# The fc products of a cross-attention block, split twice into seven: quarters of quarters for three of four groups

## The chip, the cores and the metric

The kernel runs on one core of a Trainium2 chip. The metric is the time of one launch on the device in microseconds, as the median of several runs. A separate profiled execution gives the trace from which the lines below are taken; its span is the time from its first to its last instruction. TensorE is called PE in the profile, its weight loads PEld, VectorE DVE, ScalarE ACT and GpSimd POOL; SP is the engine that issues almost all transfers. All data are fp32.

## What is computed

There are B = 8 sequences of 256 tokens with D = 512 features, a context of the same shape, 16 heads of 32, and an inner width of 2048.

```
x   = layer_norm(hidden) ;  q = x @ q_w + q_b ;  k, v = enc @ k_w + k_b, enc @ v_w + v_b
att = softmax(q k^T / sqrt(32) + mask) v
hidden = att @ cproj_w + cproj_b + hidden
y   = layer_norm(hidden)
out = hidden + gelu(y @ fc_w + fc_b) @ proj_w + proj_b
```

The change concerns the last two lines only, and of those above all y @ fc_w, a product of a 512-token group [512 x 512] with fc_w [512 x 2048].

## The kernel before

The sequences are worked through in NG = 4 groups of two sequences, that is 512 tokens. The first half of the kernel does attention for all groups; it ends at about 356 us of the trace, and nothing in it is changed but the order in which three pieces of fc_w are asked for. The second half, the `with ExitStack() as mlp` block, runs group by group: fc with gelu, then proj, then the next group. The order of all instructions on each engine is the order in which the Python code issues them (`tc.manual_schedule`); each engine works through its own queue strictly in that order, and semaphores hold an instruction until what it reads is written and what it overwrites has been read.

Large matrix products are done in Winograd's form of Strassen's method. Both operands are cut into four quarters, four sums of quarters are formed for each (`A_SUMS` on weights: s1, which takes the place of "21", s2, s3, s4; `B_SUMS` on activations: t1, t2, t4 and one that takes the place of "12"), and the four quarters of the result come from seven products instead of eight. The seven products of an operand pair are, in the order in which they are issued: ("11","11") into bank 1, ("s2","t2") into bank 6, ("s3","12") into bank 7, ("21","t1") into bank 5, then ("12","21") added into bank 1, ("22","t4") added into bank 7 and ("s4","22") added into bank 5. u1 is a copy of bank 1 on ScalarE after the first product; u2 = bank 6 + u1, u3 = bank 7 + u2, and the quarters 22, 12 or 21 are bank + u, all on VectorE. Because banks 1, 7 and 5 are added into a second time, their first contents must have been read before the second product may start in them.

In the fc part (`for q in range(HF // 2)`), fc_w lies in four pieces `fcw[q]` (tag "w", four buffers), loaded once; each piece has its seven weight operands in SBUF. For each q there are seven products of four matmuls, each of a 128x128 weight tile and 256 moving columns, all recorded under line 922, the helper `mm`; every such fp32 matmul is two instructions in the trace, so 4 x 7 x 4 x 2 = 224 per group. The names in the profile are pf for these results and fcw and y for their operands. Gelu (line 985) goes from the bank or from h into h; h holds the quarters "11", "12", "21", "22" and "s3" as lists of four tiles.

The proj part is one more Strassen product per group, h times proj_w, with seven products of 16 matmuls (results py, weights pw and pw_t). Its sums over h are made on GpSimd (lines 1026, 1027, 1078 and 1087). Between the proj products the next group's normalised tokens are transposed (pyt, lines 216 and 244, `turn_next`), and its `B_SUMS` are made on VectorE (line 171). The output grows in `ht` (named resm), which starts as the residual, and is stored by `store`.

Of the kernel before, what the change touches and what calls it, by code (L numbers as in the profile page):

```python
# [16 lines left out]
P = 128  # L17
# [5 lines left out]
def tile_xattn_block(  # L23
# [225 lines left out]
    with ExitStack() as att:  # L249
# [549 lines left out]
        for q in range(3):  # L799
            begin(g, 0, 3, load_fc, q)  # L800
# [105 lines left out]
    with ExitStack() as mlp:  # L906
        wpool = mlp.enter_context(tc.tile_pool(name="mlpw", bufs=1, reuse_waits="tile"))
        work = mlp.enter_context(tc.tile_pool(name="mlpwork", bufs=2, reuse_waits="tile"))
# [5 lines left out]
        )  # L914

# [5 lines left out]
        def mm(ps, lhsT, rhs, first, last):  # L921
            nc.tensor.matmul(ps, lhsT, rhs, start=first, stop=last, skip_group_check=True)  # L922

# [5 lines left out]
        def sum_pw():  # L929

            for to, a, b, op in (
# [5 lines left out]
                for p in range(0, HF, 2):  # L937
                    c = slice(p, p + 2)
                    nc.vector.tensor_tensor(pw[to][:, c], pw[a][:, c], pw[b][:, c], op)
                    yield  # L940
# [3 lines left out]
        nc.gpsimd.tensor_tensor(pbd, projb[:, :HD2], projb[:, HD2:], ALU.subtract)  # L944

        for g in range(NG):
            y = ys[g]

            h = {
                n: [  # L950
                    work.tile([P, 2, S], F32, tag=f"h{n}", bufs=HF // 2, name=f"h{n}_{g}_{q}")
                    for q in range(HF // 2)
                ]
                for n in ("11", "12", "21", "22", "s3")
            }

            def fc(bank, w, b, q, first, last):
                for i in range(2):
                    for c in range(HC):
                        mm(  # L960
                            bank[:, i, :],
                            fcw[q][w][:, c, ts(i, P)],
                            y[b][:, c, :],
                            first and i == 0 and c == 0,
                            last and c == HC - 1,
                        )
# [5 lines left out]
            def by_tiles(row):  # L972
                return row[:, None, :].to_broadcast([P, 2, HD2])

            for q in range(HF // 2):
                bank = {
                    n: ps_f.tile([P, 2, S], F32, tag=f"f{n}", name=f"pf{n}_{g}_{q}") for n in (1, 6, 7, 5)
                }
                u1 = work.tile([P, 2, S], F32, tag="u1", bufs=1, name=f"u1_{g}_{q}")
                u2 = work.tile([P, 2, S], F32, tag="u2", bufs=2, name=f"u2_{g}_{q}")  # L980
                u3 = work.tile([P, 2, S], F32, tag="u3", bufs=1, name=f"u3_{g}_{q}")

                def gelu(n, half, src):
                    for i in range(2):
                        nc.scalar.activation(  # L985
                            h[n][q][:, i, :],
                            src[:, i, :],
                            AF.Gelu_apprx_tanh,
                            bias=col(c_fcb, half * HF + 2 * q + i),
                            scale=1.0,  # L990
                        )

                ahead = g == 0 and q + 1 < HF // 2

                def some_pw(n):
                    if g == 0 and q:
                        for _ in range(n):
                            next(pw_sums)

                fc(bank[1], "11", "11", q, True, False)  # L1000
                nc.scalar.copy(u1, bank[1])  # L1001
                fc(bank[6], "s2", "t2", q, True, True)
                nc.vector.tensor_tensor(u2, bank[6], u1, ALU.add)
                fc(bank[7], "s3", "12", q, True, False)
                nc.vector.tensor_tensor(u3, bank[7], u2, ALU.add)
                fc(bank[5], "21", "t1", q, True, False)
                nc.vector.tensor_tensor(h["22"][q], bank[5], u3, ALU.add)
                if ahead:
                    sum_up(nc.gpsimd, fcw[q + 1], A_SUMS, 0, 1)
                some_pw(1)  # L1010
                fc(bank[1], "12", "21", q, False, True)

                gelu("11", 0, bank[1])
                gelu("22", 1, h["22"][q])
                fc(bank[7], "22", "t4", q, False, True)
                nc.vector.tensor_tensor(h["12"][q], bank[7], u2, ALU.add)
                if ahead:
                    sum_up(nc.gpsimd, fcw[q + 1], A_SUMS, 2, 3)
                some_pw(2)
                gelu("12", 1, h["12"][q])  # L1020
                fc(bank[5], "s4", "22", q, False, True)
                nc.vector.tensor_tensor(h["21"][q], bank[5], u2, ALU.add)  # L1022
                some_pw(1)
                gelu("21", 0, h["21"][q])

                nc.gpsimd.tensor_tensor(h["s3"][q], h["11"][q], h["21"][q], ALU.subtract)  # L1026
                nc.gpsimd.tensor_tensor(h["21"][q], h["21"][q], h["22"][q], ALU.add)
                if q == 0:
                    ht = residual(work, hid_dram[g], "resm", f"resm_{g}")
                    if g + 1 < NG:  # L1030
                        load_hid(g + 1)
# [6 lines left out]
            if g + 1 < NG:  # L1038
                seen, roots, normalise = layer_norm(hids[g + 1], f"m{g + 1}")
                for f in (*seen, roots, *normalise):  # L1040
                    f()
# [108 lines left out]
```

## Time and profile before

| quantity | value |
| --- | --- |
| median of 3 runs | 754.42 us (753.89 to 755.68) |
| the profiled execution: time, span | 754.31 us, 752.5 us |
| fc of group 0, of group 1, of group 2 | 48.35, 48.34, 48.35 us |
| proj of group 0, of group 1 | 50.30, 50.21 us |
| bytes moved by DMA | 68.70 MB |

Busy time on PE counts overlapping matmuls once, so a PE that is always busy need not be at its best pace. In the rows of groups, the number after x counts instructions, then come the busy time in microseconds and the mean nanoseconds of one, then the idle time of the engine just before them with what ended it. The duration of a matmul runs from its issue to its last result; matmuls overlap, so the time between two starts is shorter.

### The profile page before, as it was taken

The page shows a single profiled execution, that of the slowest core. Times are in us where ns is not written, and L with a number is a line of the kernel's source. Part 1 is how long each engine was busy: PE and PEld are TensorE (multiplying, and loading weights), DVE is VectorE, ACT ScalarE, POOL GpSimd, SP SyncE. Part 2 cuts the span into 40 slices and gives each one's busy share as a digit, 9 for nine tenths or more (in the row PEclk, how much of TensorE's full clock was granted, in tenths as well). Part 3 has the DMA queues.
Part 4 walks back from the last instruction along what each step waited for, and adds up shares of the span by engine and source line. Part 5 has one row for each costly group of instructions (what it writes and reads, how often), then busy time and mean ns, then how long its engine had stood idle before and what let it go on. Part 6 is the DMA issues. An engine that isn't in the chain of part 4 may idle for free.

```text
span 752.5 us, 12116 instructions
## 1 busy us (share of the span) xinstructions
PE 744.8 (99%) x4437; PEld 626.2 (83%) x4437; DVE 360.5 (48%) x969; ACT 293.1 (39%) x852; POOL 380.0 (50%) x346
## 2 busy tenths in 40 slices
PE   9999999999999999999999999999999999999997
PEld 7888777888888877778888888888888888888886
DVE  3676755676466566765355542245422355122111
ACT  2276777766676777761341002330013300032100
POOL 3856779577564478996654421136202165012540
PEclk9999999999999999999999999999999999999999
DMA  9614432542233267433930003000040000200001
GB/s 297 238 58 145 155 95 88 182 158 71 86 120 137 99 182 240 154 112 108 300 110 1 1 29 140 1 1 0 1 167 1 1 1 0 89 25 0 1 1 56
DMA packets 60331, 68.70 MB, mean 91 GB/s; under 512 B 5060, under 2 KB 46064, under 8 KB 60144
## 3 DMA queue, kind: packets, MB, share of 16 engines
q1 hardware_dynamic: 60016, 67.91, 27.6%
q8 instruction: 35, 0.57, 0.3%
q14 instruction: 24, 0.20, 0.1%
q0 software_dynamic: 256, 0.02, 0.0%
HBM read 46.95 MB, written 20.97 MB: 90 GB/s over the span
## 4 chain that ended last, share of the span: by engine, by line
PE 94%; ACT 2%; DMA 2%; DVE 1%; issue 0%; SPq 0%; DVEq 0%
PE py L922 26%; PE pf L922 26%; PE ppt L625 7%; PE pqT L367 6%; PE pv L367 6%; PE s L572 5%; PE po L367 5%; PE pkT L367 5%; PE av L641 5%; PE pkT L464 2%; ACT pr L600 1%; PE pyt L216 1%; PE pxt L216 1%; PE pct L216 1%; DMA kw<-in_L_xattn_k_w_dram 1%; ACT pt L630 1%
## 5 line engine op out<-in xcount | busy, mean ns | idle before, releaser
L922 PE MATMUL pf<-y,fcw 128*128 128x256 f32 x896 | 194.0, 379 | 0.0
L922 PEld LDWEIGHTS pf<-y,fcw 128*128 128x128 f32 x896 | 170.3, 190 | 23.1
L614 POOL TENSOR_TENSOR pr<-pr,rsum 128x512 f32<-128x512 f32 x128 | 130.2, 1047 | 74.9 <-DVE rsum L612 43.7
L600 ACT ACTIVATE pr<-pr,nmax 128x256 f32<-128x256 f32 x256 | 128.2, 503 | 61.3 <-DVE nmax L590 61.2
L1026 POOL TENSOR_TENSOR hs<-h,h 128x512 f32<-128x512 f32 x16 | 20.3, 1271 | 192.4 <-PE pf L922 146.7
L590 DVE CUSTOM_DVE_ANT_0 pr<-s,mb 128x256 f32<-128x256 f32 x256 | 94.0, 412 | 42.1 <-PE s L572 35.0
L922 PE MATMUL py<-pw,h 128*128 128x256 f32 x384 | 85.1, 380 | 0.0
L922 PE MATMUL py<-pw_t,h 128*128 128x256 f32 x384 | 83.5, 379 | 0.0
L922 PEld LDWEIGHTS py<-pw,h 128*128 128x128 f32 x384 | 72.7, 190 | 9.9
L922 PEld LDWEIGHTS py<-pw_t,h 128*128 128x128 f32 x384 | 72.8, 190 | 9.7
L1001 ACT COPY u<-pf 128x512 f32<-128x512 f32 x16 | 9.4, 585 | 166.3 <-PE pf L922 165.2
L625 PEld LDWEIGHTS ppt<-ident,pr 128*128 128x128 f32 x512 | 57.3, 141 | 14.8 <-issue 10.2
L625 PE MATMUL ppt<-ident,pr 128*128 128x128 f32 x512 | 68.7, 276 | 0.2
L630 ACT COPY pt<-ppt 128x512 f32<-128x512 f32 x96 | 51.6, 570 | 4.9 <-PE ppt L625 4.9
L985 ACT ACTIVATE h<-h,cols 128x256 f32<-128x256 f32 x96 | 43.4, 501 | 25.5 <-DVE h L1022 13.3
L367 PE MATMUL pv<-vw,ctxT 128*128 128x256 f32 x224 | 52.4, 380 | 0.0
L985 ACT ACTIVATE h<-pf,cols 128x256 f32<-128x256 f32 x32 | 13.4, 470 | 99.9 <-PE pf L922 99.9
L367 PE MATMUL pqT<-xnT,qw 128*128 128x256 f32 x224 | 51.1, 380 | 0.0
L600 ACT ACTIVATION_READ_ACCUMULATOR pr<-pr,nmax 128x1 f32 x256 | 48.5, 189 | 0.0
L367 PEld LDWEIGHTS pqT<-xnT,qw 128*128 128x128 f32 x224 | 41.3, 190 | 5.2 <-POOL ctxT L171 0.2
L367 PEld LDWEIGHTS pv<-vw,ctxT 128*128 128x128 f32 x224 | 41.0, 190 | 5.4 <-POOL ctxT L171 0.3
L641 PE MATMUL av<-pt,v 128*32 128x256 f32 x512 | 38.7, 386 | 1.4 <-ACT pt L630 0.4
(132 smaller groups left out, 967.0 us busy)
## 6 DMA issues: line engine op xcount, KB each, us to landing
ctx<-in_ctx_dram SPq DMA_DIRECT2D x16, 256.0 KB, 4.9
x<-in_x_dram SPq DMA_DIRECT2D x16, 256.0 KB, 4.6
v_dram<-st_v SPq DMA_DIRECT2D x16, 256.0 KB, 2.2
v<-v_dram SPq DMA_DIRECT2D x16, 256.0 KB, 3.5
resx<-in_x_dram SPq DMA_DIRECT2D x16, 256.0 KB, 5.2
hid_dram<-resx SPq DMA_DIRECT2D x16, 256.0 KB, 2.3
hm<-hid_dram SPq DMA_DIRECT2D x16, 256.0 KB, 5.9
fcw<-in_L_xattn_fc_w_dram SPq DMA_DIRECT2D x16, 256.0 KB, 6.0
```

Of the source, the lines that this page charges most:

```text
L216: nc.tensor.transpose(ps[:, ts(t, P)], xt[:, ts(c, P)], ident)
L367: nc.tensor.matmul(bank[n][:, i, :], l[:, c, ts(i, P)], r[:, c, :], start=first and i == 0 and c == 0, stop=last and c == HC - 1, skip_gro ...
L572: nc.tensor.matmul(banks[j][:, i, :], qT[j * HD : (j + 1) * HD, b * S + i * P : b * S + (i + 1) * P], kT[j * HD : (j + 1) * HD, b * SK : ( ...
L590: nc.vector.tensor_tensor_reduce(pr[:, j, i, :], banks[j][:, i, :], mbias[g][1][:, b, :], scale=-SCALE, scalar=FLT_MAX, op0=ALU.add, op1=A ...
L600: nc.scalar.activation(pr[:, j, i, :], pr[:, j, i, :], AF.Exp, bias=nmax[:, j, i : i + 1], scale=-1.0, accum_out=sums[:, j, i : i + 1],)
L614: nc.gpsimd.tensor_tensor(pr[:, j], pr[:, j], rsum[:, j, :, None].to_broadcast([P, NQ, SK]), ALU.mult,)
L625: nc.tensor.transpose(ps[:, kc, ts(i, P)], probs[n][:, j, i, ts(kc, P)], ident)
L630: nc.scalar.copy(pt, ps)
L641: nc.tensor.matmul(av[j * HD : (j + 1) * HD, :], vs[g, hg][:, b * NK + kc, ts(j, HD)], pts[n, j][:, kc, :], start=(kc == 0), stop=(kc == N ...
L922: nc.tensor.matmul(ps, lhsT, rhs, start=first, stop=last, skip_group_check=True)
L985: nc.scalar.activation(h[n][q][:, i, :], src[:, i, :], AF.Gelu_apprx_tanh, bias=col(c_fcb, half * HF + 2 * q + i), scale=1.0,)
L1026: nc.gpsimd.tensor_tensor(h["s3"][q], h["11"][q], h["21"][q], ALU.subtract)
```

## The change

Group 0 is computed as before, but its h tiles get another layout ([P, 2, 8, P] for each of the five names, so that two token halves are apart). While it runs, the seven weight operands of fc_w are themselves cut into quarters, and for each the four sums of those quarters are made (`split_sums`, 14 calls of four adds, on VectorE or GpSimd, through the three slots of a `stage` tile). Sums and original quarters (`keep_quarters`) are written to `w2_dram`, 7 x 7 pieces, 12.8 MB. The `stage` tile shares the tag "y2", with one buffer, with the later y2 tiles.

For groups 1 to 3 each of the seven outer products is done as seven inner products (`product` and `sub`), 49 in all, where a plain scheme would have 64 and the kernel before has 28 of twice the columns and the same number of matmuls each. An inner product is four matmuls of a 128x128 weight tile and 128 moving columns. The operands of one outer product (1.8 MB) come from `w2_dram` by `load_w2` into the four buffers of tag "w", four products ahead. The activations' second-level sums are made by `split_y` on VectorE.

The outer combination is no longer made in u tiles: the results of the outer products are added in place in h's buffers. `product(k, base, to)` forms base + its own result in `to`. Where there is a base, `prepare` first adds base and u on GpSimd into the target block, and `made` then adds the bank on VectorE. Five of the seven calls have a base, and between products 4 and 5 `both_to` adds whole quarters to others, half the blocks on GpSimd and half on VectorE. Gelu is then run in place from h to h, two tiles after each inner product.

In proj the sums of h are rearranged: s1, s2 and s4 stand for the former ones, and three of the products have other operands and another order; banks 1 and 5 have two buffers.

```
-        for q in range(3):
+        for q in (0, 2, 1):
             begin(g, 0, 3, load_fc, q)
...
+        def split_sums(eng, n, r):
+            a, b = fcw[r][n], fcw[r + NQF // 2][n]
+            st = stage[:, stages[0] % 3]
+            stages[0] += 1
+            s1, s2, s3, s4 = (st[:, i, :] for i in range(4))
+            add(eng, s3, a[:, 0, :], b[:, 0, :], ALU.subtract)
+            add(eng, s2, b[:, 1, :], s3, ALU.subtract)
+            add(eng, s1, s2, a[:, 0, :])
+            add(eng, s4, a[:, 1, :], s2, ALU.subtract)
+            to = w2_dram[QI[n]][:, :, r * S : (r + 1) * S]
+            nc.sync.dma_start(to[:, 2, :], s1)
+            nc.sync.dma_start(to[:, 4:7, :], st[:, 1:, :])
...
+        def load_w2(g, k):
+            t = wts.tile([P, 7, HC, S], F32, tag="w", bufs=4, name=f"w2_{g}_{k}")
+            t = t.rearrange("p i h s -> p i (h s)")
+            nc.sync.dma_start(t, w2_dram[QI[FC_ORDER[k][0]]])
...
+                    def sub(n, w, b, first, last):
+                        if first:
+                            bank[n] = bank_of(n, f"pf{n}_{k}").rearrange("p i (j s) -> p (i j) s", j=2)
+                        for m in range(HF // 2):
+                            mm(
+                                bank[n][:, m, :],
+                                wt[:, QI[w], ts(m, P)],
+                                y_of(b),
+                                first and m == 0,
+                                last,
+                            )
+                        some_gelus()
...
+                    def prepare(cd, x):
+                        if base:
+                            add(GP, block(to, cd), block(base, cd), x)
+
+                    def made(cd, n, x):
+                        add(V, block(to, cd), bank[n], block(to, cd) if base else x)
+
+                    sub(1, "11", "11", True, False)
+                    u1 = u(1)
+                    nc.scalar.copy(u1, bank[1])
+                    sub(6, "s2", "t2", True, True)
+                    u2 = u(2)
+                    add(V, u2, bank[6], u1)
+                    prepare("21", u2)
+                    prepare("12", u2)
+                    sub(7, "s3", "12", True, False)
+                    u3 = u(3)
+                    add(V, u3, bank[7], u2)
+                    prepare("22", u3)
+                    sub(5, "21", "t1", True, False)
+                    made("22", 5, u3)
+                    sub(1, "12", "21", False, True)
+                    if base:
+                        add(V, block(to, "11"), bank[1], block(base, "11"))
+                    else:
+                        nc.scalar.copy(block(to, "11"), bank[1])
+                    sub(7, "22", "t4", False, True)
+                    made("21", 7, u2)
+                    sub(5, "s4", "22", False, True)
+                    made("12", 5, u2)
+                    if k + 4 < 7:
+                        load_w2(g, k + 4)
+                    elif g + 1 < NG:
+                        load_w2(g + 1, k - 3)
+
+                def both_to(to, x):
+                    for eng, cd in ((GP, "21"), (V, "22"), (GP, "12"), (V, "11")):
+                        add(eng, block(to, cd), block(to, cd), block(x, cd))
+
+                product(0, None, "21")
+                product(1, "21", "11")
+                gelu("11", 0)
+                ht = residual(work, hid_dram[g], "resm", f"resm_{g}")
+                load_next()
+                product(2, None, "22")
+                product(3, "21", "21")
+                product(4, "21", "12")
+                both_to("21", "22")
+                both_to("22", "12")
+                product(5, "21", "21")
+                gelu("21", 0)
+                gelu("22", 1)
+                product(6, "12", "12")
+                some_gelus(len(gelus))
+                gelu("12", 1)
+                for which in ("s3", "s2"):
+                    for q in range(NQF):
+                        sum_h(which, q)
+                bias_ht()
...
+            proj(bank[1], "11", "11", True, False)
+            add(V, u1, bank[1], by_tiles(projb[:, HD2:]))
...
+            proj(bank[7], "s3", "12", True, False)
...
+            proj(bank[1], "12", "21", False, True)
...
             turn_next(0)
             turn_next(1)
...
+            proj(bank[6], "21", "t2", True, True)
...
             turn_next(2)
             turn_next(3)
...
+            proj(bank[3], "12", "22", True, True)
...
+            proj(bank[5], "11", "t1", True, True)
...
+            if g + 1 < NG:
+                split_y(g + 1)
             proj(bank[7], "22", "t4", False, True)
```

In group 0, `split_sums` for the first half of each operand is issued after the third and fourth q, together with `keep_quarters`, and for the second half between the proj products, ahead of the first four calls of `load_w2`.

## Prediction

> **What bounds the kernel now.** I read the page's engine line, then the chain that ended last, then its costliest groups.
>
> ```profile
> PE 744.8 (99%) x4437; PEld 626.2 (83%) x4437; DVE 360.5 (48%) x969; ACT 293.1 (39%) x852; POOL 380.0 (50%) x346
> ...
> PE 94%; ACT 2%; DMA 2%; DVE 1%; issue 0%; SPq 0%; DVEq 0%
> ...
> L922 PE MATMUL pf<-y,fcw 128*128 128x256 f32 x896 | 194.0, 379 | 0.0
> L922 PEld LDWEIGHTS pf<-y,fcw 128*128 128x128 f32 x896 | 170.3, 190 | 23.1
> L625 PEld LDWEIGHTS ppt<-ident,pr 128*128 128x128 f32 x512 | 57.3, 141 | 14.8 <-issue 10.2
> ```
>
> TensorE is busy throughout and is 94% of the chain; the fc products (pf) wait for nothing (idle 0.0). A matmul's 379 ns is latency: 896 of them take 194.0 us, one per 216 ns. Next, the stages of the tail (fc of group 0, its proj, fc of group 1, its proj), as busy time by stretch:
>
> ```profile
> 355.58:403.93 48.35, 48.35 (x226) 42.58 (x225) 21.30 (x31) 16.49 (x35) 25.86 (x21) 1.00 0.51 167
> 403.93:454.23 50.30, 50.30 (x241) 44.24 (x241) 25.05 (x33) 0.91 (x2) 21.63 (x17) 1.00 0.03 11
> 454.23:502.57 48.34, 48.34 (x225) 42.58 (x225) 13.82 (x20) 15.20 (x34) 7.62 (x6) 1.00 0.15 55
> 502.57:552.78 50.21, 50.21 (x242) 44.24 (x241) 21.92 (x27) 0.91 (x2) 21.63 (x17) 1.00 0.03 11
> ```
>
> Columns after the stretch: its length, then PE, PEld, DVE, ACT, POOL busy, clock, DMA. fc costs 48.35 us a group with no gap. DVE and POOL are mostly free: they follow PE and hold nothing up. The change gives them work that PE must wait for, so their unit prices (groups with shapes kept apart, MLP part) matter:
>
> ```profile
> L1027 POOL TENSOR_TENSOR h<-h,h 128x512 f32<-128x512 f32 x16 | 20.3, 1269 | 1.3
> L171 DVE TENSOR_TENSOR y<-y 128x512 f32<-128x512 f32 x16 | 19.7, 1262 | 0.1
> L1007 DVE TENSOR_TENSOR h<-pf,u 128x512 f32<-128x512 f32 x16 | 11.1, 691 | 16.6 <-PE pf L922 16.6
> L1001 ACT COPY u<-pf 128x512 f32<-128x512 f32 x16 | 9.4, 585 | 166.3 <-PE pf L922 165.2
> L985 ACT ACTIVATE h<-h,cols 128x256 f32<-128x256 f32 x96 | 43.4, 501 | 25.5 <-DVE h L1022 13.3 <-DVE h L1016 12.2
> ```
>
> **What the Trainium skill says.** "TensorE: Matmul & The Clock Gate", section "Back-to-back issue gap": N/2.4 + 2.5 ns for N columns. The trace agrees if each fp32 instruction streams its 256 columns twice: 512/2.4 + 2.5 = 216. So 128 columns should take 109. Its section "LDWEIGHTS (loading the stationary operand)" gives 128/1.2 = 107 ns for a weight load: close under 109. "SBUF — State Buffer", section "SBUF: two separate sides": a GpSimd operation and a DVE operation with two SBUF inputs exclude each other. The trace agrees: the y sums, alone 0.68, take up to 1.75 us beside GpSimd (mean 1.26), while adds with one PSUM input stay at 0.69.
>
> **Pace of the new matmuls.** No real fp32 product with 128 columns is in the trace. Bounds: 109 ns below, 190 above (the weight load's whole duration, nothing overlapped). The nearest evidence is a full fp32 weight load behind a 128-column transpose, in the timeline:
>
> ```profile
> 203.91 0.52 PEld L367 LDWEIGHTS pv<-vw,ctxT 128*128 128x128 f32 x3
> 204.02 0.60 PE L367 MATMUL pv<-vw,ctxT 128*128 128x256 f32 x2
> ```
>
> Three loads in 0.52 us, the last lasting 0.19, leave 0.33 for two intervals: 0.216 and 0.11. The matmul starts 0.11 after its load. I take 111 ns.
>
> **The change, part by part.** *Matmuls of groups 1 to 3.* Removed per group: 28 products × 4 matmuls × 2 instructions = 224 × 0.216 = 48.4 us. Added: 49 × 4 × 2 = 392 × 0.111 = 43.5. Saved 4.9 a group, **14.6** in all (17 at 109).
>
> *The new wait.* Each of seven products is seven sub-products of s = 8 × 0.111 = 0.89 us. In the five with a base (1, 3, 4, 5, 6) GpSimd prepares base + u for three blocks, in the order 21, 12, 22, and the first block DVE finishes is 22, the last prepared. That DVE add reads bank 5, into which sub-product 7 accumulates, so TensorE waits for it; the three DVE adds for 11, 21, 12 queue behind it. From the product's start: sub-product 2 is all issued at 2s = 1.78; DVE starts 0.2 later (379 ns of latency against 216 of pace, and a semaphore); u2 takes 0.69; GpSimd starts 0.08 later; three adds, 1.23 apart in a row, the last 1.27, take 3.72; 0.05, the DVE add 0.69, 0.04. Sum 2s + 5.47 = 7.25 against 6s = 5.33 when TensorE is ready: **1.9 us of wait**. The general form is 5.47 − 4s.
> Product 5 is worse. Ahead of it both_to puts four two-SBUF adds on DVE and four on GpSimd. DVE starts them after product 4's last block, 0.9 into product 5; with the port fought over they take 4 to 5 us, so u2 starts at 5.1 instead of 2.0. Sub-product 6 waits 2.1 for u3, sub-product 7 another 2.8 for GpSimd: 5.0. In product 6 two gelus stand on ACT ahead of u1 and wait for product 5's last block: u2 is 0.5 late, wait 2.4. A group: 1.9 + 2.0 + 1.9 + 5.0 + 2.4 = 13.2; three groups **+39.6**. Products 0 and 2 have no base and no wait.
>
> *Building the operands in group 0.* Splits are 14 × 4 adds of 128x256 (0.42 on DVE and 0.72 on GpSimd by L661's shape, up to 0.7 on DVE where both read SBUF). Their DMAs share SP's queue with five copies of 0.92 MB from keep_quarters. In 1 KB rows the DMA moved 345 to 355 GB/s (timed at 366:374: 351), so 4.6 MB holds the queue 13 us, and the stage slots come back late. DVE's last split of the first half waits for its slot until about 12.6 us after proj begins; v1 stands behind it, done at 15.7, and the third proj product, due at 13.8, needs its bank: +1.9. Behind v1 stand statistics (3.4), roots on GpSimd (1.3), four normalisations (1.4 each): the transposes wait +3.3. y2 shares the stage's buffer and waits for its last DMAs, themselves behind two operand loads of 1.8 MB: +3.0 in group 1's first product. Sum **+8.2**; unseen before, so bounded by −2 (proj's new order could hide a little more) and +17 (DMA at 290 GB/s, landings 0.5 us later).
>
> *Costed at nothing.* Operand loads: 12.85 MB a group, 5.3 us each, issued three products (20 us or more) ahead; SP's store, resm and hid transfers stand behind waits that end by then. The gelus' ACT time (0.40 apart, 12.8 a group) lies beside fc or the first proj product. s1 and s4 sums on GpSimd (5 us each) have a proj product of 6.9 as cover; without it +1 each. The fc_w load order (0, 2, 1) precedes use by far. The new proj order ends in one add and one store as before. split_y (four adds, 4.3) lies beside the last proj product.
>
> **Sum**: −14.6 + 39.6 + 8.2 = +33.2. The profiled execution took 754.31 (span 752.5 plus 1.8), against the median 754.42: 787.6, said as **788**.
>
> **Rivals.** (1) *Weight loads set the pace.* For it: 107 against 109 leaves no slack, and a load lasts 190. Against it: the 0.11 above. At 141 (the transposes' load) fc is 392 × 0.141 = 55.3 and the waits shrink to 5.47 − 4 × 1.13 = 0.96 in four products and 3 in product 5: 62.1 a group, +41 plus 8 gives 803; at 190, 75 a group, 842. (2) *Waits hidden: faster.* If a GpSimd prepare cost 0.6 us or less, or DVE finished another block first, 5.47 − 4s falls to zero; then −14.6 + 8.2: 748, or 740 with a free boundary. From 0.6 us an add it decides so; all 16 of L1027 are at 1.26 to 1.27, and DVE's order is written out. (3) *The clock drops or DMA is late*: the first of these pages, "Part 1: The HAM clock gate", lets an idle window of 3.4 us halve the clock; no run here shows it. Some 2 us lost in each of four or five long waits, with the boundary's upper bound: 800 to 815. That the products are not halved at all is excluded: the changed instruction order shows the 128-column matmuls.
>
> **How the numbers follow.** Likeliest case (waits behind GpSimd, pace near 111) 0.80, its own range 776 to 803; rival 1 0.09; rival 3 0.05; rival 2 0.05; 0.01 for something near zero. Slower by over 0.2% (about what a measurement of this kernel tells from no change): 0.93; within: 0.02; faster: 0.05. Range 772 to 812: it takes in the likeliest case, rival 3 and the milder half of rival 1.
>
> **What would show it.** Right: fc of groups 2 and 3 at 56 to 58 us with PE idle before pf's second pass into bank 5, released by DVE, DVE in turn by POOL; POOL prepares at 1.27; matmuls 111 apart between waits; proj of group 0 at 53 to 58. Wrong: fc below 48 (rival 2), a pace over 120 with no idle (rival 1), waits on w2's DMAs, or a clock under 1.00.

## The result and the profile after

The changed kernel takes **810.23 us** (median of 4 runs, 808.85 to 812.24), the kernel before 754.31 (4 runs, 753.89 to 755.68): 1.074 of it, with an interval of 1.0713 to 1.0767. The forecast of 788 had the side and the wait behind GpSimd; it was 22 us too low, and the result lies just inside the upper end of its range of 772 to 812, but outside the 776 to 803 of its likeliest case. The profiled execution took 808.85 us with a span of 807.0, so the spans differ by 54.5. One execution of all those below, in section 6, took 1259 us at a granted clock of 0.56, and no figure here counts it.

The page of the kernel after: the engine line, the granted clock in 40 slices, the chain that ended last, and groups (count, busy time, mean nanoseconds, idle time ahead and what ended it). The helper `mm` is line 924 here and `add` is 927.

```profile
PE 755.3 (94%) x4941; PEld 648.0 (80%) x4941; DVE 443.7 (55%) x1085; ACT 299.3 (37%) x867; POOL 473.0 (59%) x431
...
PEclk9999999999999999999999999899998799998999
...
PE 76%; POOL 10%; DVE 8%; DMA 2%; ACT 2%; issue 2%; SPq 0%; DVEq 0%; POOLq 0%
...
L924 PE MATMUL pf<-y,w 128*128 128x128 f32 x1176 | 151.8, 294 | 38.2 <-DVE h L927 27.7
L924 PEld LDWEIGHTS pf<-y,w 128*128 128x128 f32 x1176 | 147.5, 208 | 42.4 <-DVE h L927 30.8
...
L927 POOL TENSOR_TENSOR h<-h,u 128x512 f32<-128x512 f32 x45 | 55.7, 1267 | 146.3 <-DVE u L927 146.3
...
L927 DVE TENSOR_TENSOR h<-pf,h 128x512 f32<-128x512 f32 x60 | 38.7, 686 | 52.0 <-POOL h L927 45.6
```

Three things stand here that the page of before lacks. The pf matmuls had no idle time and have 38.2 us. POOL and DVE together are 18% of the chain, where POOL was not named. And the clock line has digits under 9, all of them in the fc stages. The last is easily read past: PE is still "94% busy", but a matmul instruction at half the clock counts as busy for twice as long.

The stages, as the stretches of the changed part: proj of group 0, fc of group 1, its proj, fc of group 2, fc of group 3. Columns as before: length, then busy PE, PEld, DVE, ACT, POOL, granted clock, DMA.

```profile
403.63:461.84 58.21, 52.93 (x241) 45.58 (x240) 44.09 (x54) 1.02 (x3) 46.05 (x45) 0.94 0.73 247
461.84:526.61 64.77, 49.60 (x393) 48.00 (x392) 34.93 (x48) 14.80 (x33) 25.70 (x21) 0.92 0.76 279
526.61:576.71 50.10, 50.10 (x242) 44.22 (x241) 23.82 (x33) 3.30 (x8) 25.89 (x22) 1.00 0.13 48
576.71:639.98 63.27, 51.72 (x393) 50.46 (x392) 31.08 (x44) 14.92 (x33) 26.53 (x22) 0.88 0.59 216
...
690.93:752.33 61.40, 49.92 (x393) 48.67 (x392) 31.09 (x44) 14.92 (x33) 26.36 (x22) 0.91 0.31 116
```

Against 48.35 and 50.3 before, the three fc stages lose 16.4, 14.9 and 13.1 us and group 0's proj 7.9. In the second row PE is busy for 49.6 of 64.8 us: 15 are spent waiting. But 49.6 is itself more than the 43.9 that 392 instructions take at the new pace. The wait list of the same trace (waited for, us in total, times, longest) names who ended the waits:

```profile
PE pf L924 <- DVE h L927: 27.7, 15, 2.1
PE pf L924 <- DVE u L927: 6.5, 3, 2.2
PE py L924 <- DVE v L927: 4.6, 1, 4.6
PE pf L924 <- DVE y L927: 2.7, 1, 2.7
PE pf L924 <- DVE resm L927: 1.4, 1, 1.4
PE pyt L216 <- DVE hm L203: 0.7, 1, 0.7
```

The fifteen waits for h are one in each of the five products with a base, in three groups; the three for u are u3 in product 5. Products are counted from 0 to 6, as in `product(k, ...)`. The chain of waits through one such product (group 2, product 3), start and duration, shows the mechanism from end to end:

```profile
601.49 0.70 DVE u L927
602.23 0.09 issue
602.32 0.73 POOL h L927
603.05 0.50 issue
603.55 2.49 POOL h L927 x2
606.06 0.70 DVE h L927
606.81 4.59 PE pf L924 x24
```

u2 is ready at 602.19, GpSimd's three additions run to 606.04, only then can DVE add bank 5 into block 22, and 50 ns after that addition TensorE starts again, 1.9 us after it had run dry.

**What the clock did.** The next fence has four stretches of group 2 in the form of the stages: running, a wait, the 2.7 us behind it, and running again. Compare the number of matmul instructions, in brackets after the PE busy time, and the clock (third figure from the end).

```profile
585.20:587.90 2.70, 2.70 (x27) 2.70 (x26) 1.20 (x2) 0.00 (x0) 1.76 (x2) 1.00 0.98 404
588.25:590.60 2.35, 0.24 (x3) 0.04 (x1) 0.72 (x2) 0.00 (x0) 1.60 (x2) 0.98 0.46 193
591.02:593.72 2.70, 2.70 (x14) 2.70 (x14) 1.44 (x3) 0.25 (x1) 0.00 (x0) 0.50 0.00 0
600.00:602.70 2.70, 2.70 (x27) 2.70 (x26) 1.40 (x3) 0.58 (x1) 0.38 (x1) 1.00 1.02 384
```

27 instructions fit into 2.7 us ahead of the wait, 14 behind it, at a clock of 0.50. PE is 100% busy in both. All through the fc stages the instructions start either 0.112 us apart or 0.212 to 0.216; 34, 56 and 45 of them are of the second kind in groups 1, 2 and 3. Of these 135, 11 stand alone, most of them directly behind a wait. Such a single slow start follows even gaps of 0.4 us in runs whose clock is 1.00 (section 7), so only the other 124, in stretches of five or more, are put to the clock here.

Not every wait brings such a stretch, and the lengths of the waits hardly differ. What differs is where they lie. In the clock record of this trace each stretch of half clock lasts 3.41 or 6.83 us, and their starts (590.50, 607.57, 624.63, 638.28 in group 2) lie whole multiples of 3.41 us apart. So the next fence cuts the trace at this grid. Its first two rows are the window that holds the whole wait of product 3 in group 2 and the window behind it. The other three are around the wait of product 3 in group 1, which is as long (1.86 us each) but falls across two windows.

```profile
604.16:607.57 3.41, 1.55 (x14) 1.36 (x13) 1.51 (x3) 0.00 (x0) 1.87 (x2) 1.00 1.08 450
607.57:610.98 3.41, 3.41 (x18) 3.41 (x17) 1.07 (x2) 0.58 (x1) 0.00 (x0) 0.50 0.90 269
491.51:494.92 3.41, 2.61 (x24) 2.42 (x22) 0.66 (x1) 0.00 (x0) 3.41 (x3) 1.00 1.12 437
494.92:498.34 3.42, 2.36 (x21) 2.36 (x22) 2.58 (x4) 0.27 (x1) 0.28 (x1) 1.00 0.98 416
498.34:501.75 3.41, 3.41 (x33) 3.41 (x32) 1.38 (x2) 0.31 (x1) 1.95 (x2) 1.00 1.02 366
```

With 1.86 us idle in one window (3.41 less 1.55) the next ran at half clock; with 0.80 and 1.06 in two it did not. Over twelve traces (the changed kernel's and one of each variant below, from 403 us on, each cut at the grid of its own clock record), 57 of the 60 full-clock windows with 1.85 us or more of idle were followed by half clock, and 1 of the 126 with less (some idle, but under 1.85). Out of half clock it took a window with under 0.5 us of idle: all 46 of these were followed by full clock, none of the 21 with 0.56 or more.

**The account**, in us of span, from these views:

| term | predicted | measured |
| --- | --- | --- |
| work of TensorE in fc, 3 x (392 x 0.112 - 48.35) | -14.6 | -13.3 |
| waits behind additions, three groups | +39.6 | +37.5 |
| waits at group 0's boundary (last four rows of the wait list) | +8.2 | +9.4 |
| half clock in fc: 124 instructions x 0.102 | 0 | +12.6 |
| half clock in proj: ten instructions in group 0 (2.3), stages of groups 2 and 3 (0.85 and 1.0) | 0 | +4.2 |
| rest: the 11 single slow starts (1.1), the last proj stage (0.9 longer in run 1 too, where fc ran at full clock), single instructions around a change of pace | 0 | +4.1 |
| sum | +33.2 | +54.5 |

The second row is six gaps a group between starts of pf instructions, less the pace (12.7 in group 2). Everything that was priced came out within 2.1 us of its price. What was not in the sum, the clock, is 17 of the 21 us missing.

### The profile page after: what moved, and what is told of

Read it like the earlier page. It is cut to its first block, busy times and chain, and to the rows that moved or that the text cites. A ratio compares the mean times of both kernels' runs of the same rounds, so it can differ in the third digit from the quotient of the medians.

```text
span 807.0 us, 13477 instructions
## 1 busy us (share of the span) xinstructions
PE 755.3 (94%) x4941; PEld 648.0 (80%) x4941; DVE 443.7 (55%) x1085; ACT 299.3 (37%) x867; POOL 473.0 (59%) x431
## 4 chain that ended last, share of the span: by engine, by line
PE 76%; POOL 10%; DVE 8%; DMA 2%; ACT 2%; issue 2%; SPq 0%; DVEq 0%; POOLq 0%
PE pf L924 18%; PE py L924 18%; POOL h L927 7%; PE ppt L625 6%; PE pqT L367 6%; PE pv L367 5%; PE po L367 5%; PE s L572 5%; PE pkT L367 4%; PE av L641 4%; POOL w_stage L927 2%; PE pkT L464 2%; DVE h L927 2%; DVE w_stage L927 1%; ACT pr L600 1%
## 5 line engine op out<-in xcount | busy, mean ns | idle before, releaser
L924 PE MATMUL pf<-y,w 128*128 128x128 f32 x1176 | 151.8, 294 | 38.2 <-DVE h L927 27.7
L924 PEld LDWEIGHTS pf<-y,w 128*128 128x128 f32 x1176 | 147.5, 208 | 42.4 <-DVE h L927 30.8
L600 ACT ACTIVATE pr<-pr,nmax 128x256 f32<-128x256 f32 x256 | 128.1, 503 | 61.4 <-DVE nmax L590 61.2
L927 POOL TENSOR_TENSOR h<-h,u 128x512 f32<-128x512 f32 x45 | 55.7, 1267 | 146.3 <-DVE u L927 146.3
L924 PE MATMUL py<-pw,h 128*128 128x256 f32 x384 | 89.0, 392 | 4.6 <-DVE v L927 4.6
L1188 ACT COPY u<-pf 128x512 f32<-128x512 f32 x21 | 12.2, 582 | 214.5 <-PE pf L924 214.5
L927 DVE TENSOR_TENSOR h<-pf,h 128x512 f32<-128x512 f32 x60 | 38.7, 686 | 52.0 <-POOL h L927 45.6
L1139 ACT ACTIVATE h<-h,cols 128x256 f32<-128x256 f32 x96 | 39.9, 497 | 66.5 <-DVE h L927 66.5
L927 POOL TENSOR_TENSOR h<-h,h 128x512 f32<-128x512 f32 x44 | 58.0, 1349 | 5.8 <-issue 4.7
L927 DVE TENSOR_TENSOR u<-pf,u 128x512 f32<-128x512 f32 x50 | 34.5, 690 | 40.8 <-PE pf L924 34.4
L924 PE MATMUL pf<-y,fcw 128*128 128x256 f32 x224 | 48.5, 379 | 0.0
```

The lines of the kernel that those rows point to most:

```text
L600: nc.scalar.activation(pr[:, j, i, :], pr[:, j, i, :], AF.Exp, bias=nmax[:, j, i : i + 1], scale=-1.0, accum_out=sums[:, j, i : i + 1],)
L927: eng.tensor_tensor(to, a, b, op)
L1139: nc.scalar.activation(h[n][:, :, p, :], h[n][:, :, p, :], AF.Gelu_apprx_tanh, bias=col(c_fcb, half * HF + p), scale=1.0,)
```

## The experiments

Theory: TensorE waits for the additions, and **these waits of about 2 us can halve the clock for the next microseconds**. The rival for the excess over the forecast is that something slows the matmuls as such in these stages (DMA or GpSimd at SBUF, weight loads), and that the waits cost only their 13 us a group. Each run below is of one edit on the kernel after unless it says otherwise; ratios are against the kernel before on the same chip.

### 1. Fill the waits

In each product with a base, nine matmuls into a spare PSUM tile stand ahead of the second pass into bank 5, which is where TensorE waits, and in product 5 ten more ahead of the second pass into bank 7. Their result is never read.

```
+                    def idle_work(n):
+                        idle = ps_m.tile([P, G], F32, tag="mm", name=f"idle_{g}_{k}")
+                        for _ in range(n):
+                            mm(idle[:, :P], wt[:, 0, :P], y_of("11"), True, True)
...
+                    if k == 5:
+                        idle_work(10)
                     sub(7, "22", "t4", False, True)
                     made("21", 7, u2)
+                    if base:
+                        idle_work(9)
                     sub(5, "s4", "22", False, True)
```

> The changed kernel, with 9 matmuls of 128 columns (18 instructions, 2.0 us) on operands that are at hand, into a bank nobody reads, ahead of sub-product 7 of each product with a base, and 10 more ahead of sub-product 6 of product 5; their results are not used. The waits on DVE and GpSimd stay, but TensorE is busy in them. If the slow stretches (matmuls 212 ns apart instead of 112) are the clock, lowered by the waits, they vanish in fc of groups 2 and 3: fc 63.3 and 61.4 come to about 57, the clock to 1.00 there, and the time falls by 10 to 17 us to about 797. If the slow stretches come from operand transfers or from the weight loads, nothing of them changes and the time is 810 or a little more.

Measured: **798.61 us** (798.2 to 799.43), ratio 1.059 [1.0574, 1.0606]: 11.6 us less than after, with more work on the same path. Groups 2 and 3:

```profile
577.19:635.30 58.11, 57.23 (x504) 56.49 (x502) 30.93 (x44) 14.81 (x33) 25.77 (x21) 1.00 0.62 236
...
685.40:743.19 57.79, 57.09 (x504) 56.49 (x503) 30.93 (x44) 14.81 (x33) 25.75 (x21) 1.00 0.33 124
```

110 instructions more, and the stage is 5.2 and 3.6 us shorter; the clock is 1.00 instead of 0.88 and 0.91. Instructions at half pace in group 2 fell from 56 to 6, each of them alone. DMA and GpSimd did as much as before, and there were more weight loads, so the rival falls. 58 us is also what the prediction had for these stages: with the clock held up, its arithmetic holds. Group 1 did not gain (64.77 to 64.91): its long waits, for y2, lie in product 0, which wasn't filled, and 20 instructions at half clock in a row follow them.

### 2. Fill them with transposes

The edit is shown against run 1. A transpose is one instruction here, so their number is doubled. If only matmuls held up the clock, it would still fall behind these waits.

```
-                            mm(idle[:, :P], wt[:, 0, :P], y_of("11"), True, True)
+                            nc.tensor.transpose(idle[:, :P], wt[:, 0, :P], ident)
...
-                        idle_work(10)
+                        idle_work(20)
...
-                        idle_work(9)
+                        idle_work(18)
```

> As the run with idle matmuls, but the places of the waits are filled with 18 and 20 transposes instead of 9 and 10 matmuls; what the transposes write is never read. Two theories of why filling helped. If the clock is held up by any instruction of TensorE, the transposes do as much: 797 to 801 us and a clock of 0.99. If only matmuls count, TensorE is busy in these places and the clock still falls after them: 806 to 813 us, clock under 0.98, matmuls 212 to 216 ns apart behind the transposes.

Measured: **798.29 us** (797.99 to 798.73), ratio 1.0584 [1.0569, 1.0598]; fc of groups 2 and 3 at 58.14 and 57.85 at a clock of 1.00. Transposes do the same as matmuls. The trace records them as MATMUL instructions, 0.109 us apart; that only matmuls hold up the clock falls for these fp32 transposes.

### 3. Take GpSimd out of the order: prepare 22 first

The order of the three preparations on GpSimd becomes 22, 21, 12, so that the block that DVE finishes first is prepared first. GpSimd then starts one sub-product later, since 22 needs u3.

```
-                    prepare("21", u2)
-                    prepare("12", u2)
                     sub(7, "s3", "12", True, False)
                     u3 = u(3)
                     add(V, u3, bank[7], u2)
                     prepare("22", u3)
+                    prepare("21", u2)
+                    prepare("12", u2)
```

> Same instructions, other order: block 22 is prepared first on GpSimd, then 21 and 12. By the same sum as in the prediction, block 22 is ready at 3s + 3.02 = 5.7 us (s = 0.896) from a product's start instead of 2s + 5.47 = 7.26, and TensorE is ready at 5.38: a wait of 0.3 to 0.4 us in products 1, 3, 4 and 6, some 3 to 5 us in product 5. fc about 50 to 52 us in groups 2 and 3, time about 778 us (770 to 788). If the number of GpSimd adds counted and not their place ahead of block 22 (GpSimd as a bound by its whole work), the time would stay within 5 us of 810.

Measured: **782.83 us** (781.15 to 785.26), ratio 1.0382 [1.0361, 1.0403]; fc of groups 2 and 3 at 53.2 and 52.8, a little above the 50 to 52 expected. The waits for h go from 27.7 us in 15 to 3.1 in 13, as expected. The one in product 5 for u3 stays and becomes longer (12.9 us in three instead of 6.5): TensorE comes there without the long wait of product 4, and DVE's four sums between the targets, which stand ahead of u2 and u3, take 6.2 us instead of 4.5 (group 2), beside four on GpSimd.

### 4. Take GpSimd out of the wait: DVE first

For block 22 DVE adds bank 5 into u3, which frees the bank, and GpSimd adds the base afterwards, with nobody waiting.

```
-                    prepare("22", u3)
                     sub(5, "21", "t1", True, False)
-                    made("22", 5, u3)
+                    if base:
+                        add(V, u3, bank[5], u3)
+                        add(GP, block(to, "22"), block(base, "22"), u3)
+                    else:
+                        made("22", 5, u3)
```

> Only block 22 of a product with a base is changed: DVE adds bank 5 into u3 in place, and GpSimd adds base + u3 into the target afterwards, so that no GpSimd add stands between sub-product 4 and sub-product 7. If TensorE's waits come from the three prepares on GpSimd (my theory), the wait of about 2.1 us falls to zero in products 1, 3, 4 and 6; in product 5, where both_to holds DVE, some 2.6 us before u3 stay. fc of groups 2 and 3 then takes 46 to 49 us instead of 63.3 and 61.4, the clock comes back to 0.97 or more, and the time is about 767 us (760 to 775). If the weight loads or the operand transfers set the pace instead, fc stays above 58 us and the time above 800.

Measured: **773.79 us** (772.28 to 774.55), ratio 1.0257 [1.0242, 1.0272]: 36.4 us less than after, by another order of two additions. In the wait list the row for h is gone; the largest that is left:

```profile
PE pf L924 <- DVE u L927: 11.8, 3, 3.9
PE py L924 <- DVE v L927: 4.8, 1, 4.8
```

fc of groups 2 and 3 is 49.6 and 49.4, above the 46 to 49 expected: the wait in product 5 is 3.9 us, not 2.6 (DVE's four sums take 6.2 us here too), and half clock follows it (0.97 in the stage). The additions move from one long wait into the next; that the chain from GpSimd to bank 5 held TensorE in four of five products is shown.

### 5. Take the sums between targets out of product 5

On top of run 4: DVE's two sums of 22 into 21 stand behind product 5, those of 12 into 22 are spread over product 6, and no GELUs are queued ahead of u1 and u2.

```
-                        some_gelus()
+                        if not (first and n in (1, 6)):
+                            some_gelus()
...
+                    some_late(1 if k == 6 else 0)
                     sub(1, "12", "21", False, True)
...
-                        add(eng, block(to, cd), block(to, cd), block(x, cd))
+                        f = lambda eng=eng, cd=cd: add(eng, block(to, cd), block(to, cd), block(x, cd))
+                        if eng is V:
+                            late.append(f)
+                        else:
+                            f()
```

In this run and the first of section 7 DVE's two sums of 12 into 22 follow product 6's own additions to 12 and so take in product 6 too; number and size of the operations are the same.

> On top of the earlier edit for block 22: no GELUs stand on ScalarE ahead of u1 and u2 of product 6, and DVE's two sums of product 4 into its target are put off (two behind product 5, one each into two places of product 6). Group 0 and its boundary are as in the kernel after. If waits behind the additions, and the half clock that follows them, are all that the fc stages lost: fc of groups 2 and 3 at 44.5 to 47 us (392 x 0.112 = 43.9 and a little), the clock there at 0.97 or more, the longest wait of TensorE in them under 1 us, and a total of 756 to 762 us, within 1% of before, since group 0's proj and the first product of group 1 still lose some 11 us. Rival: the sums put off only move the wait into product 6 or into the products that take up the target: fc at 49 us as with block 22 alone, total 770 to 774.

Measured: **760.51 us** (760.32 to 760.97), ratio 1.0084 [1.0069, 1.01]. Fc of group 2 and 3:

```profile
563.80:608.64 44.84, 44.04 (x393) 43.84 (x392) 27.49 (x40) 11.79 (x25) 22.38 (x19) 1.00 0.80 305
...
659.20:704.06 44.86, 44.04 (x394) 43.85 (x393) 27.49 (x40) 11.78 (x25) 22.41 (x19) 1.00 0.42 159
```

Busy 44.04 for 392 instructions: this is the stage without waits, 3.5 us shorter than before. The waits that are left in these two stages, 0.8 us at most, bring no half clock. So what fc lost there was waits behind additions and the half clock that follows them, and what lasts is group 0's boundary.

### 6. Group 0's boundary: the transfers' order, and the stage slots

Two edits on the kernel after. The first brings the copies of fc_w to DRAM one or two q earlier and has one operand load less ahead of the last splits:

```
+                        keep_quarters(0)
+                    if q == 1:
+                        keep_quarters(1)
+                        keep_quarters(2)
...
-                        for k in range(3):
-                            keep_quarters(k)
...
-                load_w2(1, 1)
...
+                load_w2(1, 1)
                 load_w2(1, 2)
                 load_w2(1, 3)
```

> Only the transfers around group 0 are placed otherwise: the quarters of fc_w are copied to DRAM one or two q earlier, and only the first of the four operand loads stands ahead of the last splits. Theory: the 5.0 us wait ahead of the third proj product of group 0 (DVE held by a stage slot behind the copies) and the waits of 2.9 and 1.7 us in group 1's first product (y2 held by stage transfers behind the loads) go, with the half clock after them (about 3 us): 8 to 12 us less, 798 to 802. proj of group 0 falls from 58.2 to 52 to 54 us. Rival: the DVE's and GpSimd's own 56 adds for the splits hold the queue, not the transfers: then less than 3 us come back.

Measured: **805.03 us** (803.41 to 806.75), ratio 1.0679 [1.0658, 1.07]: 5.2 us less than after, not 8 to 12, with proj of group 0 at 57.45 where 52 to 54 were expected. Of the 4.9 us between the two spans, 0.8 lie in that proj and 2.7 in fc of group 1; the rest lies in stages that the edit does not touch. v1's wait fell from 4.6 to 1.6 and y2's from 2.7 to 0.4, but the transposes' rose from 0.7 to 2.4.

The second makes the same additions and moves the same bytes, but the transfers read fc_w itself, so that no stage slot is waited for (groups 1 to 3 then compute with quarters in place of the sums):

```
-            nc.sync.dma_start(to[:, 2, :], s1)
-            nc.sync.dma_start(to[:, 4:7, :], st[:, 1:, :])
+            nc.sync.dma_start(to[:, 2, :], a[:, 0, :])
+            nc.sync.dma_start(to[:, 4:6, :], a)
+            nc.sync.dma_start(to[:, 6, :], b[:, 0, :])
```

> The kernel after, with one edit in group 0: the transfers of the splits read quarters of fc_w in place of the sums in the stage buffer, so the same bytes go to DRAM and the same additions are made, but no addition waits for a stage slot (the operands of groups 1 to 3 are then not the sums: that part is left out). If the late slots are what group 0's proj loses: the wait ahead of its third product, 5.0 us, falls under 1 us, the half clock behind it goes, the wait for y2 in group 1's first product (2.9) goes too, and the total is 798 to 802 us, proj of group 0 at 53 to 55. If it is the additions themselves (each 0.8 to 1.5 us while DVE and GpSimd both read SBUF): waits of 2 us and more remain there, 804 to 808 us.

Measured: 798.38 us (798.08 to 799.38, three executions), ratio 1.0591 [1.0575, 1.0607]. The trace is from a second run of the same kernel:

> The run without slot waits again, for its trace (in the first its three undisturbed times were 798 to 799, as the theory of the late slots has it). Slots: no wait over 1 us in group 0's proj and none for y2 in group 1's first product, proj at 53 to 55, 798 to 802 us. Additions: waits of 2 us and more remain there, and the gain lies elsewhere.

Measured: **799.74 us** (797.61 to 800.94), ratio 1.0601 [1.0586, 1.0616], 10.5 less than after. Proj of group 0:

```profile
403.61:456.04 52.43, 50.69 (x242) 44.14 (x241) 45.54 (x56) 1.01 (x3) 46.04 (x45) 1.00 0.52 181
```

DVE and POOL are as busy as in the kernel after (45.5 and 46.0 against 44.1 and 46.1), and the stage is 5.8 us shorter, at a clock of 1.00; the rows for v and y are gone from the wait list. So the late slots were what v1 and y2 waited for. The additions are left, and with them 1.7 us that the transposes still wait. 2.0 of the 9.2 us between the two spans lie in fc of group 2, which the edit does not touch: in the clock record four windows of half clock fall there instead of five. The trace of the kernel after shows the blocked queue (DVE; start, duration, idle time and releaser in brackets):

```profile
411.35 0.94 DVE L927 TENSOR_TENSOR w_stage<-fcw,w_stage 128x256 f32<-128x256 f32 x1
417.98 0.43 DVE L927 TENSOR_TENSOR w_stage<-fcw,fcw 128x256 f32<-128x256 f32 x1 [5.70 <-POOL w_stage L927]
...
421.46 0.68 DVE L927 TENSOR_TENSOR v<-py,projb 128x512 f32<-128x512 f32 x1
```

POOL is named since its split waited for a transfer in its turn. v1, whose bank had long been ready, stands behind the split.

### 7. Everything together

Run 5 with the first edit of section 6:

> The previous kernel with the earlier edit of group 0 as well (the copies to DRAM one or two stages earlier, one more operand load behind the last splits). If the two losses are independent, as their places say, the gain of 5 us seen for the second edit adds: 750 to 756 us, so at most 0.6% faster than before and perhaps no different; proj of group 0 at 56 to 58 us, fc of groups 1 to 3 at 48, 46 and 46. Were group 0 free of loss too, the arithmetic of the products alone would give 740. Rival: once fc no longer waits, its DMA loads or GpSimd's adds meet at the boundary and give the 5 us back: 757 or more.

Measured: **754.86 us** (13 runs, 754.04 to 756.62), ratio 1.0009 [1.0001, 1.0018]: the gains add (760.5 less 5.6), fc of groups 1 to 3 at 47.8, 44.8 and 44.9, proj of group 0 at 56.8. The kernel is level with the one before.

Next, DVE makes its sums of 22 into 21 inside product 4, and those of 12 into 22 one after product 5 and one in product 6, each ahead of what changes its operand; and the split of 22 in the second half goes to DVE. In this run an extra copy of bank 1 by ScalarE overwrites block 11 in the products with a base, all but product 4.

> The two edits (block 22 on DVE first; group 0's copies earlier) with the order of the sums between targets settled: the sums of 22 into 21 are issued inside product 4, behind its last readings of 21; DVE's sums of 12 into 22 stand at the end of product 5 and in product 6 ahead of its addition for block 11. Of group 0's last three splits, DVE takes 22. If DVE's place in the queue was all that was left in fc (1.1 us in product 6): fc of groups 2 and 3 at 44 to 45 us; y2's additions start some 2 us sooner, so the first product of group 1 loses about 1 us instead of 3. Total 749 to 753, faster than before by 0.2 to 0.7%. Rival: the sums inside products 4 and 5 delay DVE's own additions there, and TensorE waits in those instead: fc at 45.5 to 47, total 755 or more.

Measured: **751.54 us** (751.28 to 751.87), ratio 0.9966 [0.9954, 0.9978]; fc at 44.99 in all three groups, proj of group 0 at 58.1. The next run is the same without the extra copies, which are twelve, not fifteen. The fence has what both runs change in the placing of the sums and splits:

```
                 product(3, "21", "21")
-                product(4, "21", "12")
-                both_to("21", "22")
+                product(4, "21", "12", lambda: both_to("21", "22"))
                 both_to("22", "12")
...
-                for n in ("s3", "s4", "22"):
-                    split_sums(GP, n, 1)
+                for e, n in ((GP, "s3"), (V, "22"), (GP, "s4")):
+                    split_sums(e, n, 1)
```

> The run before with ScalarE's copy of bank 1 again in the products without a base alone: the whole of the computation. The copy was 15 operations of 0.58 us on an engine that waits, so fc should not move: 750 to 753 us, faster than before by 0.1 to 0.5%, fc of groups 2 and 3 at 44 to 45 us, clock 0.99 or more. Rival: without the copy GELUs come forward on ScalarE and stand ahead of u1: fc at 46 and more, total 755 or more.

Measured: **752.32 us** (751.23 to 753.14), ratio 0.997 [0.996, 0.9981]. Last, one more split moved past v1:

```
                         split_sums(GP, "s4", 0)
-                        split_sums(V, "22", 0)
...
                 split_sums(GP, "12", 1)
+                split_sums(V, "22", 0)
```

> The version with both edits, the sums between targets settled and the copy in its place, with one move: DVE's last split of group 0's first half (22), which waits 2.4 us for its stage slot with v1 behind it, goes behind the splits 11 and 12 of the second half, past v1, the statistics and the normalisations. If v1's place is what proj of group 0 still loses (2.0 us of wait, 3 to 4 us of waits for the transposes, 1.5 us at half clock): proj of group 0 at 51 to 53.5 us instead of 57.2, total 745 to 749 us, 0.7 to 1.2% faster than before. Rival: the moved split holds back the stage slots of the second half, and y2 and group 1's first product wait for its transfers instead: 751 to 755.

Measured: **749.25 us** (748.63 to 751.36), ratio 0.9937 [0.9923, 0.995]. It is 0.6% faster than the kernel before, just above the 745 to 749 expected. This version computes the whole. Its proj of group 0 and fc of group 1:

```profile
403.96:459.01 55.05, 50.91 (x242) 44.06 (x241) 48.08 (x62) 1.01 (x3) 40.73 (x41) 1.00 0.63 217
459.01:504.00 44.99, 44.30 (x393) 43.92 (x392) 31.02 (x43) 11.77 (x25) 23.31 (x19) 1.00 0.96 374
```

and what TensorE still waits for in the changed part:

```profile
PE pyt L216 <- DVE y L244: 2.8, 1, 2.8
PE pf L924 <- DVE u L927: 1.7, 3, 0.6
PE py L924 <- DVE pw_t L927: 1.3, 1, 1.3
```

Proj missed its 51 to 53.5: v1's wait is gone, but the moved split's four additions now stand ahead of DVE's copies out of the transposes' bank (y, line 244), and the next transposes wait 2.8 us for that. The wait moved once more, at a smaller size.

## Why the prediction was right, and where it was off

- **The side and the waits were right; that the number fell inside the range was in part luck.** 810.23 is beyond the 776 to 803 of the likeliest case, and one of the four runs (812.24) is beyond 812. The range reached that far for rival 3 and half of rival 1; the second did not happen, and the first was priced too low. Two of the prediction's own signs spoke against it: fc of groups 2 and 3 took 63.3 and 61.4 us, not 56 to 58, and the clock there was 0.88 and 0.91, not 1.00.
- **Work of TensorE**: 111 ns an instruction from two intervals between weight loads; 112 measured. The stage without waits is 44.0 us busy, against 43.5. Rival 1 (weight loads at 141 or 190) is out: their durations of 208 overlap.
- **Waits behind GpSimd**: the sum 2s + 5.47 gave 1.9 to 2.0 in three products, 2.4 in product 6 and 5.0 in product 5; less the pace, the gaps in group 2 are 2.3 in product 1, 2.0 in products 3, 4 and 6, and 2.3 + 2.0 in product 5. Run 4 shows the cause by taking GpSimd out of it, run 3 by its order alone. In product 6 the prediction blamed two GELUs for 0.5 us; its wait is no longer than the others, and that term was too big.
- **Boundary**: the sum was near, its parts were not. v1 waited 4.6, not 1.9; the transposes 0.7, not 3.3, since TensorE came to them that much later; y2 and the residual 4.1, not 3.0. The named cause, stage slots late behind the copies in SP's queue, is shown by both edits of section 6.
- **What failed is the term for the clock.** It stood in rival 3, which let some 2 us be lost in each of four or five long waits and got a chance of 0.05; the likeliest case had no such term. Rival 3's 800 to 815 is also more than its own terms give: 788, 8 to 10 for these waits and up to 9 for the boundary are 796 to 807. Its premise came from the Trainium skill's "TensorE: Matmul & The Clock Gate", "Part 1: The HAM clock gate", which names an idle window of 3.4 us, and no wait in fc was priced that long. Here waits of 2 us brought half the clock: 124 instructions at 0.214 instead of 0.112 in fc, 17 us in all with proj. The measurement decides. The traces do show windows of 3.41 us, but 1.85 us of idle in one of them was enough, so that each of the six waits a group that the prediction itself listed could have such a stretch behind it. Run 1 shows that it is the idle time that does this.
- Rival 2 (hidden waits, 740 to 748) was not this kernel, but it is what the edits made: with bank 5's reader moved off GpSimd and the boundary partly cleared, 749.25.

## What to carry to other kernels

When fewer operations on the matmul engine are paid for with additions elsewhere, ask of each PSUM bank that is accumulated into a second time who reads it and what that reader waits for: here an order of additions that lets DVE release the bank before GpSimd adds the base was worth 36 us. A wait of TensorE costs its length, and then the slow stretch that may follow it: here the gaps of 2 us cost a third more than their length (12.6 us on 37.5). Read the clock column beside the busy time. And an instruction that may wait for a buffer on its way to DRAM does not belong in a queue ahead of one that frees a bank.

## What the runs showed of the hardware that was not expected

- In fc, TensorE's starts are 0.112 us apart or 0.212 to 0.216, nothing lasting between: full or half clock. A wait of 2 us is followed by anything from one such instruction to a stretch of 16 (3.4 us), and the stretch may begin after a few at full pace (behind the wait of product 3 in group 2: one slow, five fast, sixteen slow). After gaps of 0.4 to 1.1 us between starts in fc of groups 2 and 3 (runs of sections 5 and 7) one slow start came, with the clock at 1.00.
- In these traces the clock changes on a grid of 3.41 us. It was halved for the next window where TensorE had idled for about 1.85 us or more, 54%, of one (57 of 60, and 1 of 126 with less), and given back after a window with under 0.5 us of idle (46 of 46). So two waits of nearly the same length can differ: one that falls inside a window halves the clock, one that is split between two need not.
- Filling a wait of 2 us with nine matmuls or eighteen transposes whose results nobody reads keeps the clock at 1.00.
- In the kernel after, an addition of 128x256 with both inputs in SBUF takes 0.41 to 0.43 us on DVE when GpSimd is idle, mostly 0.8 to 0.95 beside one of the same size on GpSimd, and 1.4 to 1.5 beside one of 128x512.
